# Layer 1's attention scores computed twice, the exponentials made with the keys on the partitions

## The chip, the cores and the metric

The kernel runs on one core of one Trainium2 chip. The core has a tensor engine (PE in the profile; PEld is its loading of weights), a vector engine (DVE), a scalar engine (ACT), a general-purpose engine (POOL) and a queue that issues most transfers (SP). The first four take their instructions in order, each from a queue of its own, and wait for one another by semaphores. The metric is the device time of one execution, in microseconds. The median of two runs before the change is 2357.4 us (2357.12 to 2357.68).

## What is computed

The program holds two transformer layers over 8 sequences of 512 positions and width 256, all in float32. Layer 0 has a recurrent attention and eight experts of which each position uses one. The change lies in layer 1: an attention of 16 heads of 16 columns with a bias by distance, and a weighted sum of eight small experts.

```python
qkv = x @ W_attn.T + b_attn
q, k, v = jnp.split(qkv, 3, axis=-1)          # then 16 heads of 16 columns
att = jnp.einsum('bhqd,bhkd->bhqk', q, k) * (1.0 / math.sqrt(D))
att = att + rel_bias                          # by distance and head
att = jnp.where(causal[None, None], att, -jnp.inf)
att = jax.nn.softmax(att, axis=-1)
y = jnp.einsum('bhqk,bhkd->bhqd', att, v)
...
for e in range(E):
    out = out + weights[:, e:e + 1] * (x @ expert_w[e] + expert_b[e])
```

## The kernel before

Layer 0 runs first, up to some 1450 us; its last part overlaps the first projections of layer 1. Layer 1 then runs one loop over `n`, sixteen steps for each of the eight sequences (`b`, called batches below). The heads of a batch go in four groups `c` of four heads. The sixteen columns of a head, padded to 32 rows by a neighbour that is multiplied by zero, lie on the partitions of `qT` and `kT`, so that the four heads of a group use four separate bands of 32 rows of the array at once. A group takes four steps, one for each tile of 128 positions.

`scores(b, c, i)` multiplies query tile `i` with all keys up to it, so that the queries lie on the partitions and the width is 128 to 512 (L1141). `qT` holds minus a quarter of q, so the products are negated scores. For each head DVE adds the negated bias and the causal mask from `strips` and takes the least of each row, `low` (L1150), and ACT makes the exponentials `pr` (L1155). Four steps later `turn(b, c, j)` transposes the 128 x 128 blocks of `pr` that have key tile `j`, so that the keys come to lie on the partitions (L1167); DVE copies two heads' blocks from PSUM to `prT` and ACT the other two (L1176, L1174). Another step later `weigh` multiplies them with the values, to which a column of ones is added for the sum of each row (L1188), and gathers four key tiles in one PSUM bank, which DVE copies out as `yTc` (L1195).

Two chains of other work are spread over the steps as a list `side` of pieces with due times. `prologue(b + 1)` normalises the next batch's rows and makes its q, k and v (L238, L245, L313, L330). `tail(b - 1)` divides the weighted sums, projects them (L1214 to L1246), normalises, makes the gate's weights (L1255 to L1291), and calls `experts(i)` for each tile of 128 rows: eight products on PE (L1303), which DVE multiplies by the weights and sums in `accd` (L1308), then POOL multiplies and adds the residual (L1312, L1313), and SP writes the rows out.

The order of each engine's queue is that of the program, arranged by a planner; `tc.issue_after(step)` puts what follows behind the step's last score product. So PE's queue has, for each step: scores, the transposes of `turn`, the products of `weigh` for the step before, and the side pieces that are due. PSUM has eight banks, of which `bank()` hands out the next free one: four are taken by the scores of a step, four by its transposes, one is held by the weighted sums, and the side pieces need up to five.

## Time and profile before

| quantity | value |
|---|---|
| median of the runs | 2357.4 us |
| profiled execution | 2365.3 us |
| its span | 2363.4 us |
| PE busy in the span | 1772.9 us (75%) |
| DVE busy | 1604.5 us (68%) |
| ACT busy | 1076.1 us (46%) |
| POOL busy | 642.7 us (27%) |
| layer 1's loop of score products | 1456.2 to about 2255 us |
| transposes of exponentials (L1167) on PE | 1280, mean 295 ns |

The profile is one execution. Its page gives the busy time of each engine, then the span in 40 equal slices with the busy tenths of each, then the costliest groups of instructions. A line of a group reads: line of the kernel, engine, operation, what is written and read, shapes, count, busy time and mean duration, and the idle time of the engine just before with what ended it. Lines in order of time read: start, duration, engine, line, operation, names, shapes, count, and in brackets idle time and what ended it. Matmuls overlap and their ends are modelled, so the distance from one group's start to the next group's start says more on PE than the durations.

### The profile page before, as it was taken

The page shows a single profiled execution, that of the slowest core. Times are in us where ns is not written, and L with a number is a line of the kernel's source. Part 1 is how long each engine was busy: PE and PEld are TensorE (multiplying, and loading weights), DVE is VectorE, ACT ScalarE, POOL GpSimd, SP SyncE. Part 2 cuts the span into 40 slices and gives each one's busy share as a digit, 9 for nine tenths or more (in the row PEclk, how much of TensorE's full clock was granted, in tenths as well). Part 3 has the DMA queues.
Part 4 walks back from the last instruction along what each step waited for, and adds up shares of the span by engine and source line. Part 5 has one row for each costly group of instructions (what it writes and reads, how often), then busy time and mean ns, then how long its engine had stood idle before and what let it go on. Part 6 is the DMA issues. An engine that isn't in the chain of part 4 may idle for free. (4 is left out here: it accounts for less than half of the span.)

```text
span 2363.4 us, 32128 instructions
## 1 busy us (share of the span) xinstructions
PE 1772.9 (75%) x10874; PEld 1215.8 (51%) x10874; DVE 1604.5 (68%) x4608; ACT 1076.1 (46%) x2579; POOL 642.7 (27%) x796
## 2 busy tenths in 40 slices
PE   6450006569677896869877797999989999999996
PEld 3220004448566685658656685554545454555543
DVE  2499999988998899899651003666666666665653
ACT  3561004455355543523332235774737374646521
POOL 0211006334472544644336633000000101010111
PEclk8675558579888998879977998999999999999997
DMA  5010000057422682248866883000000000000000
GB/s 187 16 47 0 0 0 6 18 193 269 148 72 96 215 290 80 78 168 311 234 115 202 250 299 101 1 4 21 3 21 4 21 3 21 3 21 6 10 10 9
DMA packets 83444, 209.91 MB, mean 89 GB/s; under 512 B 10248, under 2 KB 59568, under 8 KB 67664
## 3 DMA queue, kind: packets, MB, share of 16 engines
q0 software_dynamic: 28848, 157.42, 19.8%
q1 hardware_dynamic: 54432, 50.45, 7.5%
q8 instruction: 86, 1.41, 0.2%
q14 instruction: 78, 0.64, 0.1%
HBM read 175.10 MB, written 32.74 MB: 88 GB/s over the span
## 5 line engine op out<-in xcount | busy, mean ns | idle before, releaser
L1155 ACT ACTIVATE pr<-sc,low 128x384 f32<-128x384 f32 (+3 forms) x512 | 255.8, 556 | 269.5 <-DVE low L1150 267.9
L943 PE MATMUL ps<-hTs,w 128*128 128x128 f32 x1920 | 245.8, 289 | 51.0 <-ACT hTs L935 32.5
L1150 DVE CUSTOM_DVE_ANT_0 sc<-ps,strips 128x384 f32<-128x384 f32 (+3 forms) x512 | 226.6, 485 | 64.6 <-PE ps L1141 51.6
L943 PEld LDWEIGHTS ps<-hTs,w 128*128 128x128 f32 x1920 | 234.3, 203 | 65.4 <-ACT hTs L935 46.6
L540 DVE TENSOR_REDUCE state<-terms 128x16 f32<-128x272 f32 x512 | 227.3, 444 | 15.7
L961 PE MATMUL ps<-w,act 128*128 128x256 f32 x960 | 223.0, 386 | 18.7 <-DMA w<-in_wrows,idx 15.5
L551 DVE TENSOR_TENSOR state<-state,upd 128x256 f32<-128x256 f32 x511 | 220.6, 432 | 17.2
L1303 PE MATMUL ps<-ew,hTd 128*128 128x512 f32 x512 | 230.7, 604 | 0.0
L546 DVE TENSOR_TENSOR upd<-K,state 128x256 f32<-128x256 f32 x511 | 214.0, 419 | 14.9
L536 DVE TENSOR_TENSOR terms<-state,K 128x256 f32<-128x256 f32 x512 | 214.8, 419 | 12.0
L952 ACT ACTIVATE act<-ps,w 128x128 f32<-128x128 f32 x480 | 137.2, 369 | 184.9 <-PE ps L943 108.2
L1308 DVE SCALAR_TENSOR_TENSOR accd<-ps,wtd,accd 128x256 f32<-128x256 f32 x256 | 123.6, 483 | 120.1 <-PE ps L1303 74.3
L961 PEld LDWEIGHTS ps<-w,act 128*128 128x128 f32 x960 | 181.7, 194 | 44.6 <-issue 16.7
L1167 PE MATMUL ps<-cst,pr 128*128 128x128 f32 x1280 | 192.3, 295 | 12.8 <-DVE low L1150 10.6
L1167 PEld LDWEIGHTS ps<-cst,pr 128*128 128x128 f32 x1280 | 148.7, 149 | 87.1 <-issue 35.9
L1312 POOL TENSOR_TENSOR accd<-accd,bc_g 128x256 f32<-128x256 f32 x32 | 23.3, 729 | 559.3 <-DVE accd L1308 559.3
L1303 PEld LDWEIGHTS ps<-ew,hTd 128*128 128x128 f32 x512 | 95.6, 192 | 119.5 <-issue 106.0
L916 POOL DMA_INDIRECT w<-in_wrows,idx x120 | 117.5, 979 | 122.0 <-ACT act L952 90.3
L1141 PE MATMUL ps<-kT,qTc 32*128 32x384 f32 (+3 forms) x1024 | 132.2, 506 | 11.4 <-DVE v L317 6.8
L570 PE MATMUL ps<-cst,V 128*128 128x128 f32 x64 | 13.0, 385 | 169.4 <-DVE V L542 169.4
L636 POOL TENSOR_TENSOR stk<-stk,cst 128x512 f32<-128x512 f32 x96 | 119.3, 1269 | 19.0 <-ACT stk L635 16.9
L1176 DVE COPY prT<-ps 128x512 f32<-128x512 f32 (+3 forms) x256 | 117.7, 483 | 5.0 <-PE ps L1167 4.5
(238 smaller groups left out, 3024.9 us busy)
## 6 DMA issues: line engine op xcount, KB each, us to landing
hs<-zero SPq DMA_DIRECT2D x4, 1920.0 KB
hslot<-hs SPq DMA_DIRECT2D x60, 128.0 KB
ys<-ysb POOLq DMA_DIRECT2D x60, 128.0 KB, 3.8
xt<-in_x SPq DMA_DIRECT2D x16, 256.0 KB
x<-in_x SPq DMA_DIRECT2D x32, 128.0 KB
strips<-strip_d SPq DMA_DIRECT2D x16, 256.0 KB
out<-accd SPq DMA_DIRECT2D x32, 128.0 KB
wm<-in_wmod SPq DMA_DIRECT2D x2, 1536.0 KB
```

The lines of the kernel that those rows point to most:

```text
L536: nc.vector.tensor_mul(term[:, :, :HD], M, K[:, s, :].unsqueeze(1).to_broadcast([P, HD, HD]))
L540: nc.vector.tensor_reduce(delta, term, AX.X, ALU.add)
L546: nc.vector.tensor_mul(upd, K[:, s, :].unsqueeze(2).to_broadcast([P, HD, HD]), delta.unsqueeze(1).to_broadcast([P, HD, HD]),)
L551: yield nc.vector.tensor_sub(M, M, upd).ins
L943: nc.tensor.matmul(ph[:, q * P : (q + 1) * P], w[:, k * FF + f * P : k * FF + (f + 1) * P], hT[:, k, :], start=(k == 0), stop=(k == 1),)
L952: nc.scalar.activation(act[:, f, :], ph[:, q * P : (q + 1) * P], AF.Relu, bias=w[:, 2 * FF + f : 2 * FF + f + 1],)
L961: nc.tensor.matmul(py[:, :D], act[:, f, :], w[:, f * D : (f + 1) * D], start=(f == 0), stop=(f == NFC - 1),)
L1141: made = nc.tensor.matmul(pscs[r][:, :W], qT[rows, g, o, i * P : (i + 1) * P], kT[rows, g, :W], start=True, stop=True,)
L1150: nc.vector.tensor_tensor_reduce(out=sc[:, :W], in0=pscs[r][:, :W], in1=strips[:, n, S - W :], scale=1.0, scalar=3.0e38, op0=ALU.add, op1= ...
L1155: nc.scalar.activation(pr, sc[:, :W], AF.Exp, bias=low, scale=-1.0)
L1167: nc.tensor.transpose(pt[:, (i - j) * P : (i - j + 1) * P], prs[r, i][:, j * P : (j + 1) * P], ident,)
L1303: nc.tensor.matmul(pe, hT[:, k, cols], ew[:, k, e : e + 2, :], start=(k == 0), stop=(k == 1),)
```

## The change

The scores of layer 1 are computed twice. The first time is as before, but nothing is kept of it except each query's least negated score, written by DVE into one column of `lows`; the matrix `sc` is no longer read. `highest` transposes the column block `lows` on PE, so that each head's minima lie in one row, in the half of its 32 rows that q leaves empty, and subtracts that row from `qT`: for the last query tile of a group DVE does it straight from PSUM, for the others ACT negates into `high` and POOL adds. `kT` now has a one in the matching row (`bk`, and two activations with a scale in place of one), so the product of keys and queries carries the subtraction with it.

The second time is `exps`, in place of `turn`: key tile `j` against all queries from `j` on, so that the keys lie on the partitions at once. DVE adds the bias and mask from a second table, `stripsT` (32 kB on each partition, loaded in 32 pieces of 128 kB at the start of layer 1 from a scratch tensor that the setup writes), and ACT makes the exponentials in place. There are no transposes of exponentials any more.

The order of a step becomes: scores, `highest` for the step before, `weigh` for the step before, the side pieces, `exps`.

Other work changes engine. `yTc` and `wT` are copied by ACT. In `experts`, DVE keeps two of the eight terms of a tile; the other six are scaled by ACT into `term` and summed by POOL in `sums`, which POOL adds to `acc` at the end. Values are packed at 20 columns a head in place of 32, and some tiles have fewer buffers (`sc`, `yTc`, the spread gates).

```diff
+        bucketsT = sp.tile([NBUCKET, S], F32, name="bucketsT", tag="buckets")
+        nc.sync.dma_start(bucketsT, t["bucketsT"])
+        pf = bank()
+        nc.tensor.matmul(pf[:NH, :], rel, bucketsT, start=True, stop=True)
+        stripT = sp.tile([NH, STRIP], F32, name="stripT", tag="strip")
+        nc.vector.memset(stripT[:, : STRIP - S], BIG)
+        nc.vector.tensor_scalar_mul(stripT[:, STRIP - S :], pf[:NH, :], -1.0)
+        nc.sync.dma_start(
+            stripT_d, stripT.unsqueeze(1).to_broadcast([NH, COPIES_T, STRIP])
         )
...
+        bk = lq.tile([P, 2, 2], F32, name="bk", bufs=1)
+        for o in range(2):
+            nc.vector.tensor_scalar(
+                bk[:, o, :], w1["bqk"][:, 2:4], cst[:, C_EVEN + o : C_EVEN + o + 1],
+                cst[:, C_ONE + o : C_ONE + o + 1], ALU.mult, ALU.add,
+            )
...
-            vt = lq.tile([P, NT, NH, 32], F32, name=f"v{j}", bufs=1)
+            vt = lq.tile([P, NT, NH * VW + 32 - VW], F32, name=f"v{j}", bufs=1)
             nc.vector.memset(vt, 0.0)
-            nc.vector.memset(vt[:, :, :, HD : HD + 1], 1.0)
+            nc.vector.memset(by_head(vt)[:, :, :, HD : HD + 1], 1.0)
...
-        kT = lq.tile([P, 2, S], F32, tag="kT", name=f"kT{b}")
+        kT = lq.tile([P, 2, 2, S], F32, tag="kT", name=f"kT{b}")
...
-            nc.scalar.activation(
-                kT[:, g, cols], pk[:, :W], AF.Identity, bias=bqk[:, 2 + g : 3 + g]
-            )
             for o in range(2):
+                nc.scalar.activation(
+                    kT[:, g, o, cols], pk[:, :W], AF.Identity,
+                    bias=bk[:, o, g : g + 1],
+                    scale=cst[:, C_EVEN + o : C_EVEN + o + 1],
+                )
...
+        stripsT = lp.tile([P, NH, S], F32, name="stripsT", bufs=1)
+        for c in range(4):
+            first_head = 8 * (c // 2) + c % 2
+            for p0 in range(0, P, COPIES_T):
+                nc.sync.dma_start(
+                    stripsT[p0 : p0 + COPIES_T, first_head : first_head + 7 : 2, :],
+                    bass.AP(
+                        stripT_d.tensor,
+                        stripT_d.offset + first_head * COPIES_T * STRIP + P - p0,
+                        [[STRIP - 1, COPIES_T], [2 * COPIES_T * STRIP, 4], [1, S]],
+                    ),
+                )
+        lows = lp.tile([P, 2, 2, 4, 32], F32, name="lows", bufs=1)
+        nc.vector.memset(lows, 0.0)
         def scores(b, c, i):
-            kT, qT, prs = got[b]["kT"], got[b]["qT"], got[b].setdefault(c, {})
+            kT, qT = got[b]["kT"], got[b]["qT"]
             g, o = c // 2, c % 2
             W = (i + 1) * P
             pscs = [bank() for _ in range(4)]
             for r in range(4):
                 rows = slice(32 * r, 32 * r + 32)
                 made = nc.tensor.matmul(
-                    pscs[r][:, :W], qT[rows, g, o, i * P : (i + 1) * P], kT[rows, g, :W],
+                    pscs[r][:, :W], qT[rows, g, o, i * P : (i + 1) * P], kT[rows, g, o, :W],
                     start=True, stop=True,
                 )
+            at = HD * (1 - o)
             for r in range(4):
                 n = 8 * g + 2 * r + o
-                sc = lp.tile([P, S], F32, tag="sc", name=f"sc{b}_{i}_{n}", bufs=4)
-                low = lp.tile([P, 1], F32, tag="low", name=f"low{b}_{i}_{n}", bufs=8)
+                sc = lp.tile([P, S], F32, tag="sc", name=f"sc{b}_{i}_{n}", bufs=1)
                 nc.vector.tensor_tensor_reduce(
                     out=sc[:, :W], in0=pscs[r][:, :W], in1=strips[:, n, S - W :],
-                    scale=1.0, scalar=3.0e38, op0=ALU.add, op1=ALU.min, accum_out=low,
-                )
-                pr = lp.tile([P, W], F32, tag=f"pr{i}", name=f"pr{b}_{i}_{n}", bufs=6)
-                nc.scalar.activation(pr, sc[:, :W], AF.Exp, bias=low, scale=-1.0)
-                prs[r, i] = pr
+                    scale=1.0, scalar=3.0e38, op0=ALU.add, op1=ALU.min,
+                    accum_out=lows[:, o, i % 2, r, at : at + 1],
+                )
             return made.ins
-        def turn(b, c, j):
-            prs = got[b][c]
+        def highest(b, c, i):
+            g, o = c // 2, c % 2
+            pt = bank()
+            nc.tensor.transpose(
+                pt[:, :P], lows[:, o, i % 2].rearrange("p r e -> p (r e)"), ident
+            )
+            q = got[b]["qT"][:, g, o, i * P : (i + 1) * P]
+            if i == NT - 1:
+                nc.vector.tensor_sub(q, q, pt[:, :P])
+                return
+            high = lp.tile([P, P], F32, tag="high", name=f"high{b}_{c}_{i}")
+            nc.scalar.mul(high, pt[:, :P], -1.0)
+            nc.gpsimd.tensor_add(q, q, high)
+        def exps(b, c, j):
+            kT, qT = got[b]["kT"], got[b]["qT"]
+            g, o = c // 2, c % 2
             W = S - j * P
+            pscs = [bank() for _ in range(4)]
+            for r in range(4):
+                rows = slice(32 * r, 32 * r + 32)
+                nc.tensor.matmul(
+                    pscs[r][:, :W], kT[rows, g, o, j * P : (j + 1) * P], qT[rows, g, o, j * P :],
+                    start=True, stop=True,
+                )
             prTs = []
             for r in range(4):
-                pt = bank()
-                for i in range(j, NT):
-                    nc.tensor.transpose(
-                        pt[:, (i - j) * P : (i - j + 1) * P],
-                        prs[r, i][:, j * P : (j + 1) * P],
-                        ident,
-                    )
+                n = 8 * g + 2 * r + o
                 prT = lp.tile([P, S], F32, tag="prT", name=f"prT{b}_{c}_{j}_{r}", bufs=8)
-                if r % 2:
-                    nc.scalar.copy(prT[:, :W], pt[:, :W])
-                else:
-                    nc.vector.tensor_copy(prT[:, :W], pt[:, :W])
+                nc.vector.tensor_add(prT[:, :W], pscs[r][:, :W], stripsT[:, n, :W])
+                nc.scalar.activation(prT[:, :W], prT[:, :W], AF.Exp, scale=-1.0)
                 prTs.append(prT)
             return prTs
...
             W = S - j * P
             for r in range(4):
                 nc.tensor.matmul(
-                    yT[32 * r : 32 * r + 32, j * P :], v[:, j, 4 * c + r, :],
+                    yT[32 * r : 32 * r + 32, j * P :],
+                    v[:, j, (4 * c + r) * VW : (4 * c + r) * VW + 32],
                     prTs[r][:, :W],
                     start=(j == 0), stop=(j == NT - 1),
                 )
             if j == NT - 1:
-                out_T = lp.tile([P, S], F32, tag="yTc", name=f"yTc{b}_{c}", bufs=6)
-                nc.vector.tensor_copy(out_T, yT)
+                out_T = lp.tile([P, S], F32, tag="yTc", name=f"yTc{b}_{c}", bufs=5)
+                nc.scalar.copy(out_T, yT)
                 got[b].setdefault("yTs", []).append(out_T)
         def tail(b, got):
             xs, yTs = got["xs"], got["yTs"]
-            g10 = spread(lp, "g10", b)
-            g11 = spread(lp, "g11", b)
+            g10 = spread(lp, "g10", b, 1)
+            g11 = spread(lp, "g11", b, 1)
...
                 for i in range(NT):
                     nc.tensor.transpose(pt[:NE, i * P : (i + 1) * P], wt[:, i, :], ident)
                 wT = lp.tile([NE, S], F32, tag="wT", name=f"wT{b}", bufs=1)
-                nc.vector.tensor_copy(wT, pt[:NE, :])
+                nc.scalar.copy(wT, pt[:NE, :])
                 wTs.append(wT)
             def experts(i):
                 cols = slice(i * P, (i + 1) * P)
                 pb = bank()
                 nc.tensor.matmul(pb[:, :D], wTs[0][:, cols], eb, start=True, stop=True)
+                sums = lp.tile([P, D], F32, tag="sumd", name=f"sumd{b}_{i}")
+                nc.scalar.copy(sums, pb[:, :D])
                 acc = lp.tile([P, D], F32, tag="accd", name=f"accd{b}_{i}")
-                nc.scalar.copy(acc, pb[:, :D])
                 for e in range(0, NE, 2):
                     pe = bank()
                     for k in range(2):
...
                             start=(k == 0), stop=(k == 1),
                         )
                     for j in range(2):
-                        nc.vector.scalar_tensor_tensor(
-                            acc, pe[:, j * D : (j + 1) * D], wt[:, i, e + j : e + j + 1], acc,
-                            ALU.mult, ALU.add,
-                        )
+                        part, by = pe[:, j * D : (j + 1) * D], wt[:, i, e + j : e + j + 1]
+                        if (e, j) == (0, 0):
+                            nc.vector.tensor_scalar(acc, part, by, None, ALU.mult)
+                        elif (e, j) == (4, 0):
+                            nc.vector.scalar_tensor_tensor(
+                                acc, part, by, acc, ALU.mult, ALU.add
+                            )
+                        else:
+                            term = lp.tile(
+                                [P, D], F32, tag="term", name=f"term{b}_{i}_{e + j}", bufs=2
+                            )
+                            nc.scalar.activation(term, part, AF.Copy, scale=by)
+                            nc.gpsimd.tensor_add(sums, sums, term)
+                nc.gpsimd.tensor_add(acc, acc, sums)
                 nc.gpsimd.tensor_mul(acc, acc, g11)
                 nc.gpsimd.tensor_add(acc, acc, xs[:, i, :])
                 nc.sync.dma_start(out[b, cols, :], acc)
...
         STEP = 4 * NT
-        side, turned = [], None
+        side, made = [], None
         for n in range(B * STEP + NT + 1):
             b, m = divmod(n, STEP)
             if m == NT + 2:
...
             if n < B * STEP:
                 step = scores(b, m // NT, m % NT)
             with tc.issue_after(step):
-                last, turned = turned, None
+                if 0 < n <= B * STEP:
+                    b, m = divmod(n - 1, STEP)
+                    highest(b, m // NT, m % NT)
+                if made:
+                    weigh(*made)
+                while side and side[0][0] < n + 1:
+                    side.pop(0)[1]()
+                made = None
                 if NT <= n < B * STEP + NT:
                     b, m = divmod(n - NT, STEP)
-                    turned = b, m // NT, m % NT, turn(b, m // NT, m % NT)
-                if last:
-                    weigh(*last)
-                while side and side[0][0] < n + 1:
-                    side.pop(0)[1]()
+                    made = b, m // NT, m % NT, exps(b, m // NT, m % NT)
```

## The prediction

> **What bounds the kernel now.** I read the slices first. Layer 1 begins near 1450 us, PE is at 9 tenths from there nearly to the end, and its granted clock is near full, so a slower clock explains nothing.
>
> ```profile
> PE   6450006569677896869877797999989999999996
> DVE  2499999988998899899651003666666666665653
> ACT  3561004455355543523332235774737374646521
> PEclk8675558579888998879977998999999999999997
> ```
>
> The stretches by batch came next. One batch in the middle of layer 1, from one first expert tile to the next, is 112.27 us long:
>
> ```profile
> 1828.76:1941.03 112.27, 103.74 (x597) 56.45 (x596) 70.66 (x247) 63.61 (x141) 11.67 (x16) 0.95 0.04 12
> ```
>
> PE is busy in 103.74 of it, DVE in 70.66, ACT in 63.61. PE sets the pace, but its ends are modelled, so I priced PE by slots, from the start of one group to the start of the next, in the order of time. This is one step with an expert tile:
>
> ```profile
> 1851.12 0.50 PE L1141 MATMUL ps<-kT,qTc 32*128 32x128 f32 x8
> 1851.55 1.97 PE L1167 MATMUL ps<-cst,pr 128*128 128x128 f32 x16
> 1853.45 0.43 PE L1188 MATMUL ps<-prT,v 128*32 128x128 f32 x8
> 1853.81 0.69 PE L1297 MATMUL ps<-eb,wT 8*128 8x256 f32 x2
> 1854.43 7.13 PE L1303 MATMUL ps<-ew,hTd 128*128 128x512 f32 x16
> 1861.49 0.71 PE L1141 MATMUL ps<-kT,qTc 32*128 32x256 f32 x8
> ```
>
> No gap is in it: scores 0.43, transposes 1.90, weighing 0.36, experts 7.68. PE takes its queue in order: scores(n), transposes(n), weigh(n-1), side work, scores(n+1). What `weigh` reads was made a whole step earlier, so it never waits.
>
> By such slots, a group of four steps (widths 128, 256, 384, 512) costs scores 0.43+0.65+0.86+1.07 = 3.01, transposes 1.90+1.46+1.15+0.55 = 5.06, weighing 2.70: 10.8 us, and 43.1 for a batch. Side work per batch: experts 4 x 7.67 = 30.7, the prologue 11.7 (16 records of 0.44, the rest of 0.1 to 0.24), the rest of the tail 9.85. The loop of scores runs from 1456.2 to 2255.0, 798.8 us, with eight batches of scores, six of experts, seven prologues and seven tails: 8 x 43.1 + 6 x 30.7 + 7 x 11.7 + 7 x 9.85 = 679.9. So PE idles about 119 us in it.
>
> **What is removed and added.** Per batch and on PE: 160 transposes go (4 x 5.06 = 20.2 us of slots); 64 score products with keys on the partitions come (the same shapes as the present scores: 4 x 3.01 = 12.0), and 16 transposes of the minima (0.11 us each in a run, 0.3 alone: 2 to 5). By PE's work alone this gains 3 to 6 us a batch.
>
> DVE per batch: 32 copies (8 x (0.684+0.546+0.417+0.284) = 15.4) become 64 additions. Their shape is not in the trace; the nearest rows are the copies of the same width, and at 256 the addition z (423 ns) costs what the copy costs (417). So +15.4; 24 of 32 expert accumulations go (-11.6), four copies yTc and one wT go (-3.4), four subtractions come (+1.1): +1.5. ACT loses 32 copies (-13.3) and gains the same yTc and wT (+2.9), 12 negations (+3.0), 24 terms and two key activations (24 x 0.38 + 1.4 to 24 x 0.61 + 1.4, by the PSUM copy of 256 and the scaled activation xn): +3.5 to +9. POOL gains 28 additions of 0.73 and 12 of at most 0.73 (+20 to +29 on 11.7). None of these three fills 112 us, and an expert tile's terms (six on ACT, 2.3 to 3.7 us; seven POOL additions, 5.1) fit under its 7.7 us on PE. I cost them at nothing while PE is the bound; without that cover it would be a few us a batch.
>
> **The wait it adds.** In the compiled program PE's order becomes: exps(n), scores(n+1), highest(n), weigh(n), side work, exps(n+1). `weigh(n)` reads what exps(n) started: PE product, four additions on DVE, four exponentials on ACT. In between lie only one group of scores and one transpose. Behind the waiting `weigh`, in order, lie all the side work and the next exps, and for these DVE and ACT wait.
>
> The trace has a chain of the same make: scores on PE, four DVE passes from PSUM, four exponentials. Here at width 512:
>
> ```profile
> 1840.69 1.14 PE L1141 MATMUL ps<-kT,qTc 32*128 32x512 f32 x8
> 1841.85 0.69 DVE L1150 CUSTOM_DVE_ANT_0 sc<-ps,strips 128x512 f32<-128x512 f32 x1
> ...
> 1844.64 0.72 ACT L1155 ACTIVATE pr<-sc,low 128x512 f32<-128x512 f32 x1
> ```
>
> From PE's start to the last exponential's end: 1845.36 - 1840.69 = 4.67 us. At 384 it is 3.76 (1872.28 to 1876.04), at 256 2.91 (1892.07 to 1894.98), at 128 2.45 less 0.48 for a foreign accumulation in between, 1.97 (1851.12 to 1853.57). Then the fourth head's two weighing records must still run: two of 0.43 us at 512, by width 0.86, 0.64, 0.43, 0.22. So exps to the end of weigh takes 5.53, 4.40, 3.34, 2.19: 15.5 us a group where now 10.8 are spent; scores and the transpose of the minima lie inside it. That is +4.7 a group, +18.8 a batch, +150 for eight batches, if all present idle stays.
>
> Much of it will not stay, since PE now pauses at `weigh` while side results get ready. If all 119 us vanished: 8 x 61.8 + 335.1 = 829.5 against 798.8, still +31. I name what stays: yc behind the row statistics that wait for a DMA,
>
> ```profile
> 1878.27 0.43 DVE L186 BATCH_NORM_STATS2 stc<-xs 128x6 f32<-128x256 f32 x1 [2.31 <-DMA xs<-x]
> 1879.74 0.69 PE L1229 MATMUL ps<-cst,yc 128*128 128x128 f32 x2 [4.01 <-DVE yc L1219]
> ```
>
> seven times, 20.8 us in the waits; in the new kernel this DMA also queues on SP behind an output that POOL finishes some 1.7 us later. Further wtd (10.1) and the square root's two table loads, 14 pairs of 1.28 + 0.30 + 1.28 us, which now stand directly ahead of exponentials that `weigh` awaits. Some 60 of the 119 stay: +91.
>
> **Ends of the kernel.** stripsT is 4.2 MB in 32 issues on SP, ahead of the next batch's rows, and can start only when the layer 0 gate it overlies is read, at 1456.0; the first additions are due some 8 us later (the first transposes now start at 1464.1) and need 1 MB. At the 187 to 311 GB/s of the busiest slices that is 3 to 6 us, all of it 14 to 22: between 0 and 20 us of stall, and I take 3. Layer 0 keeps its order; the setup has one more small product and two more DMAs beside waits of 5 to 18 us on SP: 0 to 2, taken as 0. After the last expert tile two terms on ACT and one more POOL addition follow in a row, and the last weigh waits: +3 (1 to 5).
>
> Sum: 91 + 3 + 3 = +97. The profiled execution took 2365.3 us (span 2363.4), the runs' median 2357.4, 0.3% less: 2462 by the profiled one, **2454** by the median.
>
> **A rule against this change.** Four heads' scores at 512 leave PE in 1.07 us, while DVE needs 0.61 a head, 2.44, to read them; at present two heads' transposes go through DVE and two through ACT at once. The Trainium skill, "TensorEngine Tiling (Array Packing)", Performance Considerations, says that tiling speeds TensorE up but not the emptying of PSUM, and asks for ScalarE and VectorE to share it; the change gives all of it to VectorE. By that rule alone the pace would be DVE's own passes, some 13.5 us a group (four heads, twice 0.61+0.48+0.35+0.22, and a subtraction of 0.28); by the measured chain it is 15.5, since exponentials and weighing come behind.
>
> **Rivals.** (A) *Faster, 2290 to 2320.* If weighing found its data ready, PE would save 3 to 6 us in each of eight batches, -38, and perhaps 20 of idle: near 2300. The point: the chain must end before scores and one transpose do. They end 1.07+0.65+0.2 = 1.9 us after exps starts at width 512, 1.06 at 128; the chain needs 4.67 and 1.97. It misses at all four widths, and no side work stands between in PE's order. 6%.
> (B) *Within 2%, about 2385.* PE's pauses swallow nearly all present idle, +31 to +46. For it: most of the idle is short waits for banks and results. Against: the DMA and the table loads. 19%.
> (C) *All idle stays,* or DVE, without side work to hide behind in the first two batches (13.5 us a group on DVE alone), adds its own wait: +150 to +170, about 2520. 17%.
> (D) *The transposes stay or the loads of stripsT hold the start:* the compiled order shows no transposes of pr; the second is priced above. 2%, counted with the slower.
> The forecast, with some 40 to 80 us of idle kept, has 56%.
>
> **How the numbers follow.** 2% is 47 us, about what can be told from no change here. Slower by more: forecast, C and D, 75%; same: B, 19%; faster: A, 6%. The range takes B's centre and C: 2385 to 2525; A, B's lower half and what lies above C stay out.
>
> **What would show it.** Right: PE idle ahead of the weighing, ended by ACT's exponentials, 1 to 3 us at each of 128 steps; the twelve steps without an expert tile longer, the four with one nearly equal (15.5 + 30.7 = 46.2 us against 43.5); a middle batch near 122 us; DVE's share near 70 us a batch. Wrong: weighing without a wait, a batch below 110, or PE waiting mainly for q's subtraction, for POOL, or for stripsT. The weakest step is how much idle survives; the next, that additions cost what copies of their width do.

## The result

The changed kernel takes 2532.35 us in the median (2528.09 and 2536.61) where the kernel before takes 2357.4: a ratio of 1.073 (95% interval 1.068 to 1.078), slower by 7.3%. The forecast was 2454 us with 2385 to 2525 as its range: right in its sign, but the loss is nearly twice as large as forecast, and the time lies 7 us above the range. The profiled execution took 2528.1 us with a span of 2526.0, 162.6 more than the span before (2363.4).

The slices of the profile after, to be held against those of the kernel before: layer 1 is longer, PE stays at 8 and 9 tenths, and its clock is near full.

```profile
PE   5440036587777968698768779999989898989996
...
DVE  2499999989987998995500066646564655565631
...
PEclk8775557698979998799789979999999999999997
```

A batch in the middle, from one first expert tile to the next, in the stretches (length, then busy time of PE, its weight load, DVE, ACT, POOL, the granted clock): 129.58 us against 112.27.

```profile
1839.56:1969.14 129.58, 118.78 (x584) 56.70 (x581) 72.62 (x254) 66.79 (x152) 37.24 (x56) 0.96 0.04 11
```

Where the 162.6 us came, by the times of the score products and of the last tail's first transposes:

| stretch | before | after | more |
|---|---|---|---|
| to the first scores of layer 1 | 1456.2 | 1459.7 | 3.4 |
| to the last scores of width 512 | 795.0 | 939.6 | 144.6 |
| to the last tail (four steps without scores) | 44.1 | 57.1 | 13.0 |
| the last tail | 68.1 | 69.7 | 1.6 |

So all but 5 us lies in the eight batches' steps. The stretch from the first scores to the first expert product, where no expert work runs yet, is 40.0 us longer (193.2 against 153.2), and a middle batch some 17 to 21. In the middle batch the four steps with an expert tile take 45.9 us (1910.23 to 1956.10) where they took 43.5; the other twelve take 83.7 where they took 68.8.

One step with an expert tile of the changed kernel, width 384, in the order of time: the product of `exps` starts, DVE adds, ACT exponentiates, and PE's weight load for the weighing (L1247) starts its last pair 0.05 us after the last exponential's end (1911.82 + 1.92 = 1913.74). Only then come the experts (L1357). From the start of `exps` to there it is 4.32 us.

```profile
1910.23 0.31 PEld L1226 LDWEIGHTS ps<-qTc,kT 32*128 32x128 f32 x8 [0.22 <-issue]
...
1911.17 1.95 DVE L1234 TENSOR_TENSOR prT<-ps,stripsT 128x384 f32<-128x384 f32 x4 [1.09 <-PE ps L1226]
...
1911.82 1.92 ACT L1235 ACTIVATE prT<-prT 128x384 f32<-128x384 f32 x4 [0.91 <-DVE prT L1234]
...
1913.79 0.14 PEld L1247 LDWEIGHTS ps<-prT,v 128*32 128x32 f32 x2 [0.33 <-ACT prT L1235]
...
1914.55 0.29 PEld L1357 LDWEIGHTS ps<-eb,wT 8*128 8x128 f32 x2 [0.62 <-DVE lows L1196]
```

The steps without an expert tile are longer than this chain alone, since other work stands in the same queues of DVE and ACT. In the step that starts at 1859.56 (width 384) the tail's row statistics wait for POOL between the first and the second addition (its chain takes 5.21 us, priced at 4.40):

```profile
1861.52 0.43 DVE L203 BATCH_NORM_STATS2 std<-xs 128x6 f32<-128x256 f32 x1 [0.45 <-POOL xs L1306]
1861.86 1.01 DVE L1234 TENSOR_TENSOR prT<-ps,stripsT 128x384 f32<-128x384 f32 x2
```

In the step at 1872.50 (width 128) the additions come late, and a table load on ACT stands ahead of the exponentials; the step's chain takes 4.18 us, where 2.19 was its price:

```profile
1872.50 0.57 PE L1226 MATMUL ps<-qTc,kT 32*128 32x128 f32 x8
...
1873.81 0.87 DVE L1234 TENSOR_TENSOR prT<-ps,stripsT 128x128 f32<-128x128 f32 x4
1874.29 1.28 ACT L1235 ACT_TABLE_LOAD   x1
...
1875.58 0.91 ACT L1235 ACTIVATE prT<-prT 128x128 f32<-128x128 f32 x4
```

Added up over the sixteen steps of this batch, the chain from `exps` to what follows its weighing takes 69.2 us: 15.1 in the four steps with an expert tile and 54.1 in the other twelve. The next batches have the same 54.1 within 0.1 us.

The waits of PE's weight loads from 1456 to 2400 us (total, number, longest): the first is the wait forecast, the second PE's transpose of the minima behind DVE's additions; both stand in the chain. The third is for `yc`, the weighted sums divided by their row sums, which PE transposes in the tail. In the kernel before the first two don't exist; its largest waits for another engine are 22.9 us (the transposes L1167 behind `low`) and 22.5 for `yc`.

```profile
PEld ps L1247 <- ACT prT L1235: 96.1, 214, 2.9
...
PEld ps L1207 <- DVE prT L1234: 62.5, 87, 1.4
PEld ps L1289 <- DVE yc L1279: 30.7, 7, 6.1
```

```profile
PEld ps L1229 <- DVE yc L1219: 22.5, 7, 4.3
```

### The profile page after: what moved, and what is told of

Read it like the earlier page. It is cut to its first block, busy times and chain, and to the rows that moved or that the text cites. A ratio compares the mean times of both kernels' runs of the same rounds, so it can differ in the third digit from the quotient of the medians.

```text
span 2526.0 us, 32587 instructions
## 1 busy us (share of the span) xinstructions
PE 1902.3 (75%) x10748; PEld 1209.8 (48%) x10748; DVE 1621.0 (64%) x4669; ACT 1090.1 (43%) x2661; POOL 846.3 (34%) x1116
## 5 line engine op out<-in xcount | busy, mean ns | idle before, releaser
L1234 DVE TENSOR_TENSOR prT<-ps,stripsT 128x256 f32<-128x256 f32 (+3 forms) x512 | 219.4, 481 | 125.9 <-PE ps L1226 111.3
L1196 DVE CUSTOM_DVE_ANT_0 sc<-ps,strips 128x384 f32<-128x384 f32 (+3 forms) x512 | 249.2, 487 | 50.0 <-PE ps L1187 5.5
L1235 ACT ACTIVATE prT<-prT 128x256 f32<-128x256 f32 (+3 forms) x512 | 215.8, 467 | 123.9 <-DVE prT L1234 117.0
L973 PEld LDWEIGHTS ps<-hTs,w 128*128 128x128 f32 x1920 | 234.4, 203 | 65.1 <-ACT hTs L965 46.5
L1247 PE MATMUL ps<-prT,v 128*32 128x512 f32 (+3 forms) x1024 | 214.0, 470 | 19.2 <-ACT prT L1235 12.2
L1216 POOL TENSOR_TENSOR qTc<-qTc,high 128x128 f32<-128x128 f32 x96 | 43.7, 455 | 497.9 <-ACT high L1215 497.9
L1382 POOL TENSOR_TENSOR sumd<-sumd,term 128x256 f32<-128x256 f32 x192 | 139.1, 725 | 171.9 <-ACT term L1381 165.9
L1187 PE MATMUL ps<-kT,qTc 32*128 32x128 f32 (+3 forms) x1024 | 185.8, 492 | 14.2 <-DVE lows L1196 8.7
L1381 ACT ACTIVATE term<-ps,wtd 128x256 f32<-128x256 f32 x192 | 84.8, 471 | 164.6 <-DVE accd L1372 79.3
L1187 PEld LDWEIGHTS ps<-kT,qTc 32*128 32x128 f32 x1024 | 103.4, 199 | 75.7 <-DVE prT L1234 25.4
```

The lines of the kernel that those rows point to most:

```text
L973: nc.tensor.matmul(ph[:, q * P : (q + 1) * P], w[:, k * FF + f * P : k * FF + (f + 1) * P], hT[:, k, :], start=(k == 0), stop=(k == 1),)
L1187: made = nc.tensor.matmul(pscs[r][:, :W], qT[rows, g, o, i * P : (i + 1) * P], kT[rows, g, o, :W], start=True, stop=True,)
L1196: nc.vector.tensor_tensor_reduce(out=sc[:, :W], in0=pscs[r][:, :W], in1=strips[:, n, S - W :], scale=1.0, scalar=3.0e38, op0=ALU.add, op1= ...
L1234: nc.vector.tensor_add(prT[:, :W], pscs[r][:, :W], stripsT[:, n, :W])
L1235: nc.scalar.activation(prT[:, :W], prT[:, :W], AF.Exp, scale=-1.0)
L1247: nc.tensor.matmul(yT[32 * r : 32 * r + 32, j * P :], v[:, j, (4 * c + r) * VW : (4 * c + r) * VW + 32], prTs[r][:, :W], start=(j == 0), s ...
```

## The experiments

Four theories were put to the test. (1) The weighing's wait for additions and exponentials is the cost. (2) VectorE waits for itself: in the changed kernel each reduction starts 0.23 us after the accumulator read of the one before it, since all of them write into one buffer `sc` (four in the kernel before). (3) The expert work moved to ACT and POOL costs. (4) VectorE, which alone empties PSUM, is the bound. A fifth, on TensorE's clock, came out of the first runs. Ratios are to the kernel before, timed on the same chip; a hundredth is 23.6 us, and the intervals are two to six thousandths to each side.

| run | edit | median, us | ratio | 95% |
|---|---|---|---|---|
| | the changed kernel | 2532.4 | 1.073 | 1.068 to 1.078 |
| 1 | reductions write over PSUM | 2506.7 | 1.058 | 1.054 to 1.063 |
| 2 | weighing a step later | 2455.4 | 1.039 | 1.035 to 1.043 |
| 3 | 1 and 2 | 2437.8 | 1.030 | 1.027 to 1.034 |
| 4 | experts as before | 2512.9 | 1.063 | 1.059 to 1.066 |
| 5 | 3, half the additions left out | 2437.8 | 1.031 | 1.028 to 1.033 |
| 6 | 3 and 4 | 2437.2 | 1.028 | 1.024 to 1.031 |
| 7 | kernel before, statistics later | 2388.3 | 1.011 | 1.008 to 1.014 |
| 8 | 3, statistics later | 2467.3 | 1.043 | 1.041 to 1.045 |
| 9 | 3, idle products, two a step | 2539.9 | 1.073 | 1.069 to 1.078 |
| 10 | 3, idle products, one a step | 2471.6 | 1.044 | 1.040 to 1.048 |
| 11 | kernel before, statistics ordered | 2362.4 | 0.998 | 0.996 to 1.000 |
| 12 | 3, statistics ordered | 2432.9 | 1.028 | 1.024 to 1.032 |
| 13 | changed kernel, idle products, one | 2545.3 | 1.077 | 1.074 to 1.081 |
| 14 | changed kernel, idle products, two | 2586.9 | 1.097 | 1.093 to 1.100 |
| 15 | changed kernel, half the additions left out | 2507.6 | 1.063 | 1.059 to 1.067 |
| 16 | changed kernel, no exponentials | 2480.8 | 1.050 | 1.044 to 1.055 |

### The wait itself: runs 2, 13, 14, 16 and 15

Run 2 lets the weighing take the exponentials of two steps before:

```diff
-        for n in range(B * STEP + NT + 1):
+        for n in range(B * STEP + NT + 2):
...
-                if made:
-                    weigh(*made)
+                if kept:
+                    weigh(*kept)
...
-                made = None
+                kept, made = made, None
```

> The changed kernel, but the weighing takes the exponentials begun two steps before instead of one, so that a whole step lies between; all else is the same, and the last weighing comes one step later. Theory 1: the wait for the exponentials goes; TensorE's slots of a group become 3.01 + 3.01 + 2.70 + about 0.8 = 9.5 us where the chain took 15.5, so up to 8 x 4 x (15.5 - 10.8) = 150 us come back: 2340 to 2420 us. Theory 2: VectorE has 13.5 us of passes a group and 16 x 0.23 = 3.7 us of waits for itself, 17.2 together, more than the chain; the pace of steps without side work stays, and 2450 to 2530 us are left.

3.4 hundredths come back, 80 us, about half of the 150 that the chain was priced at. That is less than theory 1 asked for, and the time lies at the lower end of theory 2's range: the wait counts, and it is not all. Part of the gain is lost again: the loop stands at half clock for 163.8 us instead of 112.6 (below), worth up to 26. The wait for exponentials is gone from the weight loads' waits; the largest on another engine are now PE behind DVE's additions (for a PSUM bank), and yc.

```profile
PEld ps L1207 <- DVE prT L1234: 51.9, 83, 1.1
PEld ps L1289 <- DVE yc L1279: 36.4, 7, 7.3
PEld ps L1187 <- DVE prT L1234: 36.0, 58, 1.4
```

Runs 13 and 14 leave the changed kernel's order alone and put idle products in front of its wait, 96 steps of them:

```diff
             pt = bank()
+            if not 2 <= (c * NT + i + 1) % STEP <= 5:
+                for _ in range(1):          # 2 in run 14
+                    nc.tensor.matmul(pt, ident, strips[:, 0, :], start=True, stop=True)
             nc.tensor.transpose(
```

> The changed kernel (2532 us) with idle work for TensorE just ahead of the weighing's wait: in the 12 steps of each batch without an expert tile, one product of a constant with a strip, 128x128 by 512, 0.86 us by its two records in the run with the same idle work (I had counted it as 0.446 in the expectations of the two runs before). 96 x 0.86 = 83 us in all. Theory 1 (the weighing stands 1 to 3 us in each of these steps for additions and exponentials, TensorE is empty there): nearly all of it is hidden, 2520 to 2550 us. Otherwise (TensorE's own work sets the pace in these steps): 2580 to 2620 us.

> The same with two products a step, 165 us in all. Theory 1: the waits at widths 512 and 384 still hide it, those at 256 and 128 only in part; 2550 to 2590 us. Otherwise: 2660 to 2700 us.

Of 83 us put in, about 10 are paid (less than the intervals); of 165, 56. Both are in theory 1's ranges: a step takes 0.8 us for nothing of one product (73 us in 96 steps) and 1.1 of two (109). Two things paid for it. The weighing's wait for exponentials, over all of layer 1, falls from 104.6 us to 86.2 and 58.4; and the loop's half-clock time falls from 112.6 us to 81.9 and 71.7, worth up to 15 and 20. So the clock is a part of this. The other 58 and 89 us were hidden in waiting; of these the lists of waits show 18 and 46 at the weighing and 11 at the minima's transpose, and the rest has no row of its own.

Run 16 shortens the chain itself, by its last link (the line with `AF.Exp` in `exps` is deleted).

> The changed kernel without the 512 exponentials: the weighing takes the sums of scores and strips as they are (the weights are left out of the result, which is then no attention). The chain from the product to the end of the weighing ends with the fourth addition instead of the fourth exponential: shorter by one exponential (0.63 us at width 512, 0.52, 0.42, 0.30) and the hand-over to it (0.1 to 0.2), and free of what stands on ScalarE ahead of the exponentials; 2.3 to 2.7 us a group. Theory 1 (the chain's length is paid, 32 groups): 74 to 86 us less, of which the half clock may take back a third as TensorE gets less busy: 2445 to 2480 us. If the wait is for TensorE's banks or for VectorE's queue and the exponentials lie beside it: 2515 to 2540 us.

2.3 hundredths, 55 us. The median lies 0.8 us above theory 1's range; the kernel before took 2364.6 us beside it, 0.3% more than above, so by the ratio it is inside. In a middle batch (1886.58 to 2012.52) the chain takes 63.4 us instead of 69.2. The weighing now waits for DVE instead of ACT, and less: 61.0 us against 96.1.

```profile
PEld ps L1246 <- DVE prT L1234: 61.0, 126, 2.3
```

Run 15 was to shorten the chain at its other link:

```diff
-                nc.vector.tensor_add(prT[:, :W], pscs[r][:, :W], stripsT[:, n, :W])
-                nc.scalar.activation(prT[:, :W], prT[:, :W], AF.Exp, scale=-1.0)
+                if r % 2:
+                    nc.scalar.activation(prT[:, :W], pscs[r][:, :W], AF.Exp, scale=-1.0)
+                else:
+                    nc.vector.tensor_add(prT[:, :W], pscs[r][:, :W], stripsT[:, n, :W])
+                    nc.scalar.activation(prT[:, :W], prT[:, :W], AF.Exp, scale=-1.0)
```

> The changed kernel, but heads 1 and 3 of each four leave out the addition of the strip, their exponentials read the scores in PSUM (these heads' relative biases and causal mask are left out of the result). The chain from the product to the end of the weighing loses two of four additions: ScalarE's four exponentials then end it, about 0.6 + 4 x 0.63 + 0.43 = 3.6 us instead of 5.3 at width 512, by the same reckoning some 12 us a group instead of 15.5 to 16. Theory 1 (the length of this chain is what is paid): 8 x 4 x 3 to 4 = 100 to 130 us less at most, 2420 to 2470 us; the same edit gave nothing once the weighing lagged a step more. If the gain of the lag came from another order of VectorE's or TensorE's queue and not from the chain: 2505 to 2535 us.

It gave 1.0 hundredths, 23 us, in the range of the other theory. Its trace says why it tells little: the weighing still waits 79.7 us for ACT, on the exponentials that read PSUM and on those behind an addition, so the chain was hardly shorter; and the loop's half-clock time rises from 112.6 us to 153.6, which can hide up to 20 us of gain. It counts neither way.

```profile
PEld ps L1250 <- ACT prT L1238: 43.5, 64, 3.1
PEld ps L1250 <- ACT prT L1235: 36.2, 85, 1.0
```

### VectorE behind itself: runs 1 and 3

```diff
-                sc = lp.tile([P, S], F32, tag="sc", name=f"sc{b}_{i}_{n}", bufs=1)
...
-                    out=sc[:, :W], in0=pscs[r][:, :W], in1=strips[:, n, S - W :],
+                    out=pscs[r][:, :W], in0=pscs[r][:, :W], in1=strips[:, n, S - W :],
```

> The changed kernel, but the reduction that finds a head's least score writes its unused full-width output over the scores in PSUM instead of into the one buffer `sc`; so no reduction waits for the one before it. In the changed kernel each of the 512 reductions stands 0.23 us behind the accumulator read of the one before (0.85 us from start to start at width 512, 0.61 in the kernel before): 512 x 0.23 = 118 us of VectorE. Theory 1 (what costs is the weighing's wait for the additions and exponentials, 15.5 us a group of four steps whatever the reductions do, since these lie behind the additions): 2510 to 2535 us, nearly no gain. Theory 2 (VectorE's wait for itself is what keeps the old idle time alive): 2420 to 2480 us, half of the 118 or more.

> Both edits together: the weighing lags two steps, and the reductions write over the scores in PSUM. Theory 1: the same as the lag alone within 15 us, 2330 to 2410 us. Theory 2: neither edit alone helps but both together do, 2330 to 2380 us, at least 70 us below the lag alone. If both waits count, it lies 20 to 60 us below the lag alone, and then it may be below the kernel before (2357).

Run 1 gives 1.5 hundredths, 34 us (26 by the medians): theory 1 expected none to 22, theory 2 at least 52, so the truth lies between them, nearer to theory 1. Run 3 lies 18 us below run 2, 0.8 hundredths: both waits count, and neither theory alone has the numbers. The groups of the two pages show the wait for itself: DVE's idle time ahead of the reductions falls from 50.0 us to 6.0, though one reduction into PSUM takes longer (517 against 487 ns). The 118 us I had counted are a start-to-start reckoning; from 0.85 us the distance at width 512 falls to 0.65. Half-clock time falls too in run 1, from 112.6 us to 85.3; up to 14 of the 34 us may be that.

```profile
L1196 DVE CUSTOM_DVE_ANT_0 sc<-ps,strips 128x384 f32<-128x384 f32 (+3 forms) x512 | 249.2, 487 | 50.0 <-PE ps L1187 5.5
```

```profile
L1195 DVE CUSTOM_DVE_ANT_0 ps<-ps,strips 128x384 f32<-128x384 f32 (+3 forms) x512 | 235.1, 517 | 6.0 <-PE ps L1187 5.8
```

### The moved expert work: runs 4 and 6

Run 4 takes the experts' accumulation and the copies `yTc` and `wT` back to VectorE, as in the kernel before; run 6 is run 3 with the same.

> The changed kernel with the experts' part of the tail as in the kernel before: all eight accumulations of a tile and the copies yTc and wT on VectorE again, no terms on ScalarE, no additions on GpSimd. VectorE gets 11.6 + 3.4 = 15 us a batch more, ScalarE and GpSimd 12 and 20 less. Theory 3 (the moved expert work costs: the later output and row load, and the slower expert tiles at the end, +14.6 us): 2490 to 2520 us. Theory 1 (the wait for the exponentials, in which VectorE is the longest part): 2530 to 2570 us, since the accumulations stand between the additions on VectorE's queue.

> The kernel with both edits (2438 us), and the experts' part as in the kernel before: 24 accumulations and five copies a batch back on VectorE, +15 us a batch there. Theory 4 (VectorE's emptying of PSUM is what TensorE waits for now): 2440 to 2500 us, the work given to ScalarE and GpSimd was needed. Theory 3 (the moved expert work costs as it did in the changed kernel, where taking it back gave 19.5 us): 2410 to 2425 us.

In the changed kernel the old experts are 1.0 hundredths better, 24 us, as theory 3 says, though DVE is busy for about 87 us in a batch instead of 73. The path goes through POOL: POOL ends the output later, SP's load of the next batch's rows waits for that, DVE stands at the row statistics, and yc behind them. In the changed kernel's middle batch POOL ends at 1960.83, SP issues the output at 1960.87 and the load at 1961.30, the statistics wait for it until 1963.90, and yc starts at 1966.17. PE's wait for yc is 21.9 us in run 4 where it is 30.7 in the changed kernel, and the half-clock time falls from 112.6 us to 85.3, worth up to 14; the two together make 22.5. With the lag the same edit gives 0.2 hundredths, less than the intervals, and the time lies between the two theories' ranges.

```profile
PEld ps L1289 <- DVE yc L1279: 21.9, 7, 4.5
```

### What is left behind the wait: runs 5, 9 and 10

Run 5 is run 3 with the edit of run 15.

> The kernel with both edits (weighing two steps behind, reductions over the scores in PSUM; 2438 us), but heads 1 and 3 of each four leave out the addition of the strip: their exponentials read the scores in PSUM directly, so these heads' relative biases and causal mask are left out of the result. VectorE loses 256 additions of 0.28 to 0.68 us, 27 us a batch at 0.42 on the mean of four widths, and ScalarE empties a quarter of the banks of scores. Theory 4 (with the weighing's wait gone, TensorE waits for PSUM banks that VectorE alone empties; about 130 us of such waits are listed for that kernel from 1450 us on): 2370 to 2405 us. Theory 1 alone (nothing but the weighing's wait mattered, and TensorE's own work is the rest): 2425 to 2440 us.

Nothing: 1.031 against 1.030, with 87 us less of DVE time in the loop (540.2 to 453.5). Theory 4 falls, in this form: what was left was not VectorE's passes.

The granted clock is another candidate. The stretches of the loop, from the first scores to the last of width 512, of the kernels before, after, and runs 2, 3 and 10; the number behind the last bracket is the clock:

```profile
1456.24:2251.23 794.99, 737.35 (x4402) 409.58 (x4402) 513.86 (x1828) 479.55 (x1059) 80.27 (x109) 0.96 0.05 13
```

```profile
1459.65:2399.25 939.60, 857.41 (x4276) 405.17 (x4277) 550.85 (x1921) 474.12 (x1084) 242.73 (x371) 0.94 0.07 16
```

```profile
1455.95:2333.45 877.50, 780.02 (x4268) 393.29 (x4268) 547.60 (x1922) 470.82 (x1084) 242.47 (x371) 0.91 0.07 17
```

```profile
1462.08:2324.48 862.40, 779.18 (x4269) 394.21 (x4271) 540.22 (x1921) 470.12 (x1084) 242.55 (x370) 0.91 0.07 17
```

```profile
1460.12:2344.19 884.07, 818.73 (x4456) 398.06 (x4458) 544.94 (x1921) 471.50 (x1084) 243.18 (x371) 0.96 0.07 17
```

In these loops the trace's clock is either 1.00 or 0.50. Counted by its records, the time at 0.50 is 68.3 us in the kernel before, 112.6 after, 163.8 with the lag, 161.1 in run 3. At half clock an expert product starts 0.85 us after the one before it instead of 0.43, so a stretch that PE bounds loses half of its length, at most 34, 56, 82 and 81 us. Run 3's loop is 67.4 us longer than that of the kernel before; the clock can account for up to 46 of them. Time in which PE and its weight load are both empty accounts for another 25.4 (82.9 us against 57.5), half of it at yc (35.5 against 22.5); the two together are 4 us more than the loop's difference.

Runs 9 and 10 tried to buy the clock back with idle products (run 13's edit in run 3's kernel).

> The kernel with both edits (weighing two steps behind, reductions over the scores in PSUM; 2438 us), plus idle work for TensorE: in the 12 steps of each batch without an expert tile, two products of a constant with a strip (128x128 by 512, 0.446 us each by the expert products' rows) ahead of the transpose of the minima, into the same bank, overwritten by it. In all 96 x 0.89 = 86 us of TensorE work that nobody needs. Theory 5 (with the transposes gone and the wait gone too, TensorE is idle often enough in these steps for the granted clock to fall to 0.50: 161 us of the loop stand at half clock there, 68 in the kernel before, worth up to 46 us; the idle work keeps it busy): the half-clock time falls below 110 us and the time stays at 2440 us or falls, down to 2400. Theory 6 (the clock is a result of waits which the idle work doesn't touch): the half-clock time stays, and the time rises by 30 to 86 us, 2470 to 2520.

> The same with one such product instead of two, 43 us of idle work in all. Theory 5: half-clock time between that without idle work (161 us) and that with two, time 2410 to 2440 us. Theory 6: 2455 to 2480 us.

Both theories were partly wrong, and so was my size: a product is two records of 0.43 us, so the idle work is 82 and 165 us. The half-clock time did fall, from 161.1 us to 68.3 with one product and 47.8 with two, as theory 5 says; but the time rose by 1.4 and 4.3 hundredths. The sum of run 10's loop closes: 82 us of idle work, less 46 (half of 92.8 us of half clock), less 18 of empty time (82.9 to 65.1), makes 18; the loop grew by 21.7 (862.4 to 884.1). So the clock's price is real, but idle work costs more than it returns.

### The row statistics: runs 7, 8, 11 and 12

Before and after, DVE stands at the row statistics until a load lands, with yc behind them. These runs issue the load first and the statistics a step later:

```diff
-                for i in tiles:
-                    nc.sync.dma_start(xs[:, i, :], x2d[b][i])
...
+                yield lambda tiles=tiles: load(tiles)
+            yield lambda tiles=tiles: norm(tiles)
```

> The kernel before, with one edit: the row statistics of the next batch's prologue stand one step behind the issue of their rows' load instead of right behind it, so that VectorE doesn't stand at the load's landing with yc behind it. Before, TensorE waits seven times about 3 to 4 us for yc (20.8 us). If that wait ends the stretch: 2332 to 2350 us, faster than both. If another wait stands behind it (the exponentials behind the table load, or the bank of the next scores): 2352 to 2362 us, no change.

> The kernel with both edits (2438 us), and the row statistics one step behind the issue of their rows' load. TensorE waits there seven times 5 to 7 us for yc (35 us). If these waits are what is left of the moved expert work's cost: 2400 to 2415 us. If VectorE's emptying of PSUM is the pace in these steps anyhow (theory 4): 2425 to 2440 us, since VectorE has as much to do.

> The kernel before with the next batch's row statistics one step behind the issue of their load, and this time ordered on VectorE behind the last reduction of that step (in the first try VectorE's order still had them ahead of yc: TensorE's wait for yc was 20.2 us as before, and a wait of 21.7 us for hTc came on top). If the wait for yc (20.8 us, and the half-clock stretches of 6.8 us that follow it) ends: 2330 to 2350 us. If the later statistics make the prologue's products late: 2357 to 2400 us.

> The kernel with both edits (2438 us) and the row statistics ordered behind the last reduction of the step after their load's issue. TensorE stands there for yc 5 to 7 us a batch, and half clock follows for 6.8 to 13.7 us. If that wait ends: 7 x 5 = 35 us and up to 7 x 3 = 21 us of clock, 2385 to 2415 us. If the later statistics make the prologue late: 2435 to 2470 us.

None of the four went as either side expected, except run 11, which came late as its second side says. In run 7 the planner put the statistics ahead of yc all the same, and the prologue came later; runs 7 and 8 are 1.1 and 1.3 hundredths worse than the kernels that they change. Ordered behind the step's last reduction (runs 11 and 12), yc's wait falls to a third (8.1 us in run 11 instead of 22.5, 13.2 in run 12 instead of 35.5), but PE now waits for the prologue's normalised rows `hTc`, 21.7 us from 1620 to 2260 in run 11. The outcome is no change that can be measured: 0.998 and 1.028. No version tried is faster than the kernel before.

## Why the prediction was right and wrong

- **The sign and the mechanism** were right: the weighing waits for the chain begun just ahead of it. Runs 2, 13, 14 and 16 show it. The wait at the weighing itself is smaller than the "1 to 3 us at each of 128 steps" of the forecast: 104.6 us over layer 1, 0.8 a step, and 1.3 with that of the minima's transpose (63.2).
- **The chain's price** was right for the chain alone: predicted 5.53, 4.40, 3.34, 2.19 us from `exps` to the end of the weighing; in the four expert steps of a middle batch 5.40, 4.32, 3.20, 2.19. The expert steps' 46.2 us were 45.9. In the other twelve steps it was too low: 54.1 us where three groups of 15.5 make 46.4. An addition costs what a copy does: 481 ns on the mean, 483 predicted. DVE's share of a batch rose by 2.0 us (predicted 1.5), POOL's by 25.6 (20 to 29), ACT's by 3.2 (3.5 to 9 predicted, though the terms given there add up to 3.1 to 8.6).
- **The step that failed** is "Some 60 of the 119 stay: +91". The steps of the eight batches cost 144.6 + 13.0 = 157.6 us, where the chain is worth 150 if all old idle stays. A middle batch shows where the idle went. By the prediction's own slots 16.9 us of its 112.27 were idle before. After, 8.1 of its 129.58 are left outside the chain (if the side work takes as long as before), about what the 60 assumed; but the chain takes 69.2 us instead of the priced 61.8, 7.4 more. Together that is 15.5 us a batch, nearly all of the old 16.9. The prediction let PE's new pauses swallow the old waits. That would hold for PE alone; but DVE and ACT take their work in order too, and the waits of the side work (the statistics behind POOL, and the table load that the prediction had named, in the rows above) now stand ahead of additions and exponentials and lengthen the chain. One step more, at 1968.13 (width 256), takes 5.15 us instead of 3.34 at half clock. So rival C ("All idle stays", about 2520), to which I gave 17%, is what came, by the number. In part it came by costs that I had not priced: the runs put 34 us on VectorE behind itself and 24 on the moved experts, in sums that overlap with each other, with the wait and with the clock (runs 1 and 2 give 34 and 80 apart, 100 together).
- **"So a slower clock explains nothing"** was a misreading of a clock "near full". In the loop of the kernel before 68.3 us stand at half clock, so up to 34 of the 119 us were slowed work and no pause; 57.5 us were empty of PE work and weight loads. After, half clock is 112.6 us, up to 22 more of lost time. Empty time is 81.0, which counts the new waits too and so doesn't say how much of the old is left.
- **"I cost them at nothing"** was wrong for the experts. Neither ACT nor POOL became full, as argued; but the later end of POOL's chain delays a load, and that delays yc. The text had named the 1.7 us by which the output comes later and did not add what follows from it.
- **The ends**: the last tail cost 1.6 us (1 to 5 predicted). The start's 3.4 look like the 3 predicted, but that is luck: they lie ahead of the first scores, where the stall for `stripsT` can't be yet, and in runs that change nothing before that point the first scores come anywhere from 1456.0 to 1466.7. The stall, if any, is in the loop: the profile's chain of releases goes through the landing of `stripsT` at 1476.87, and the first addition starts at 1477.01. Its cost was not measured alone.
- **The rule on emptying PSUM** (the Trainium skill, "TensorEngine Tiling (Array Packing)", Performance Considerations): with the lag PE does wait for banks that the additions hold (51.9 and 36.0 us in run 2), but taking half of the additions away (run 5) gained nothing, so DVE's pace of 13.5 us a group was not shown to bind anywhere.
- **Open**: the rest of the lag kernels' loss. Half clock (up to 46 us) and yc are named by records of single profiles and by run 10's sum; why the clock falls where it does in them was not settled, nor was the load of stripsT at the start tried alone.

## What to carry over

Before pricing a new wait as "swallowed by present idle", split that idle: stretches at half clock are slowed work, not room. Ask on which engine's queue the old waits stand: if the new chain goes through that engine, they become part of it (15.1 us a group for the chain alone here, 18.0 in the other steps). A product that is used in the same step puts the whole chain through the other engines on PE's path; here a step of distance between making and using gave 80 us back, where the instructions saved on PE were priced at 3 to 6 us a batch. Look at what a scratch output's buffer count does on its own engine.

## What was not expected of the hardware

**Clock.** The granted clock halves after short pauses and stays so for 3.4 to 27.3 us in these traces from the loop's start on. In the kernel before, after 4.0 us without a product (1875.7 to 1879.7, the wait for yc in the prediction):

```profile
1874.00:1878.00 4.00, 1.73 (x15) 0.69 (x14) 1.97 (x8) 2.56 (x6) 0.94 (x2) 0.95 0.58 138
1878.00:1882.00 4.00, 2.26 (x10) 1.66 (x14) 2.98 (x12) 1.52 (x2) 0.00 (x0) 0.50 0.20 61
1882.00:1886.00 4.00, 3.95 (x24) 1.66 (x17) 2.57 (x10) 3.32 (x6) 0.00 (x0) 0.70 0.01 4
```

After, the pause is 5.6 us (from 1961.1) and the half clock lasts 10.2, in the same place of five batches in a row:

```profile
1961.00:1965.00 4.00, 0.10 (x1) 0.00 (x0) 1.10 (x5) 0.09 (x1) 0.25 (x1) 1.00 0.65 197
1965.00:1969.00 4.00, 2.35 (x14) 1.95 (x16) 2.33 (x11) 1.90 (x3) 0.00 (x0) 0.60 0.00 0
1969.00:1973.00 4.00, 4.00 (x21) 1.43 (x17) 3.15 (x11) 2.80 (x8) 0.27 (x1) 0.50 0.00 0
1973.00:1977.00 4.00, 4.00 (x26) 2.95 (x22) 2.00 (x7) 0.37 (x1) 1.20 (x3) 0.62 0.00 0
```

It also halves where there is no such pause: in the kernel before at 1536.2, with no gap above 0.13 us in the 7 us ahead, and more often in the lag kernels. In run 12 it falls at 1742, with PE or its weight load busy all but 0.16 us over the 7 us before:

```profile
1738.00:1742.00 4.00, 3.84 (x43) 2.35 (x35) 3.90 (x20) 1.92 (x8) 0.45 (x1) 1.00 0.00 0
1742.00:1746.00 4.00, 4.00 (x19) 1.73 (x18) 2.78 (x11) 1.28 (x3) 0.00 (x0) 0.52 0.00 0
1746.00:1750.00 4.00, 3.41 (x22) 1.58 (x25) 2.75 (x13) 2.68 (x6) 0.46 (x1) 0.50 0.01 4
```

The Trainium skill, "TensorE: Matmul & The Clock Gate", HAM oscillation, gives the rule that no idle gap of PE should exceed about 3.4 us. The first two cases agree with it: gaps of 4.0 and 5.6 us, and the clock fell. In the last case the rule was kept by the records and the clock fell all the same, and the measurement decides: here short products, many of them in bands of 32 rows, lost the clock with small gaps as well. Why is not settled; the ends of PE's records are modelled, so its true gaps may be longer than shown.

**VectorE behind itself.** A reduction that waits for the reduction before it (one output buffer) starts 0.85 us after it at width 512; with no such wait 0.65 in run 3 and 0.61 in the kernel before. The Trainium skill, "VectorE: DVE Perf Modes", The DRAIN you can't avoid, says of eight copies in a row that a semaphore after each costs nothing extra. For this reduction with its accumulator read, the wait cost about 0.2 us each.
